# Cross-attention with layer norm on one core: another table of slots for weight sums, scalings, loads and output steps

## The chip, the cores and the metric

The kernel runs on one core of a Trainium2 chip. The metric is the device time of one execution in microseconds (us); the core's engines are TensorE (PE, with its weight loads PEld), VectorE (DVE), ScalarE (ACT), GpSimd (POOL) and SyncE (SP, which here only issues DMAs). All data are 32-bit floats, apart from a mask of bytes.

## The reference

Eight batches of 256 query rows (x, 1024 columns) attend to 256 context rows with 32 heads of 32 columns. Cut to what is computed:

```python
x = (hidden - mu) * rsqrt(var + 1e-5) * ln_gamma + ln_beta
Q = split_heads(x @ Wq.T)              # K = V = split_heads(ctx)
scores = einsum('bhsd,bhtd->bhst', Q, K) * 32 ** -0.5
probs = softmax(where(mask, scores, -inf))
attn = einsum('bhst,bhtd->bhsd', probs, V)
out = hidden + attn.reshape(B, S, 1024) @ Wout.T
```

## The kernel before, in words

**Slots.** The work of a batch is cut into eight groups of four heads (128 columns), so there are 64 groups, and the main loop has 64 slots n = 0 to 63. What slot n issues to PE, in this order: the scores of group n+1 (L596, 16 matmuls into four PSUM banks `sc`), output steps of place 0, the product of probabilities and values of group n-2 (L780, 64 matmuls), output steps of place 1, a piece of the query projection for a coming group (L455 for batches 0 to 2, L557 later), and output steps of place 2. Each engine takes its instructions in the order in which the program issues them; engines wait for each other by semaphores. From slot 1 on a slot takes PE 6.7 to 12 us. Slot 5 begins at 58.3 us of the span, slot 6 at 65.9, slot 7 at 73.4, slot 8 at 81.0, slot 9 at 90.0, slot 17 at 157.4, slot 23 at 213.1, slot 41 at 366.3.

**Softmax of a group** (`softmax_parts`, called in slot n for group n+1). For each of four heads j and two halves of the rows: DVE reads the scores from PSUM, adds the mask and takes the minimum (L636, the scores are negated), ACT takes the exponential and its sum (L640). Then, per head, `normalize(j)`: DVE takes the reciprocals of both sums (L650), and two instructions scale the halves of the tile `e` by them, 128x256 each (L656 on POOL or DVE, L654 on ACT). A pair (n, j) of the table `scaled` names the engine, A, V or P; pairs that the table does not list are POOL's. Then `blocks(j)`: DVE transposes the tile in blocks of 32 into `pT` (L662), and ACT copies a part (`aside`, L668). The order on DVE is exponentials of heads 0, 1, 2, `normalize(0)`, those of head 3, `normalize(1)`, `blocks(0)`, `normalize(2)`, `blocks(1)`, `normalize(3)`, `blocks(2)`; in groups below 8 `blocks(3)` comes in the next slot, behind the first two reads of scores. The scores of a group go into the four banks that the group before must have left, so scores n+1 wait until DVE has read scores n. Four DMAs on SP's queue then swap parts of `pT` among partitions.

**Weights.** After the first batch the query weights are multiplied by gamma, one of eight folds for each block of 128 outputs (L476, POOL; `foldat` has the slot of each). Query product 15, which slot 8 issues, needs fold 7 of slot 7. From batch 3 on the query projection, and the output projection of all batches, use seven products of half size in place of eight (a Strassen-Winograd scheme). For this the weights are summed: T1 = B12 - B11, T3 = B22 - B12, T2 = T3 + B11, T4 = B21 - T2, each in four chunks of 128x512, for the query weights by `sum_wq` (L506, table `wq`: slot, name, chunk, engine), for the output weights by `sum_wo` (L292, table `wo`: slot, name as a number, 3 for T1 to 6 for T4, chunk, engine). Sums and folds are issued at the end of a slot, behind the slot's softmax. T1, T3 and B11 of the query weights are stored to memory (`keeps`) and loaded into a ring again for each batch (`rings`).

**Layer norm.** x is loaded, DVE takes the statistics (L341, L344, L346), POOL the power -1/2 (L349), the row block is normalised by POOL or DVE (L367) or ACT (L362, with a shift from POOL, L359); `norm2` has the engines for batch 2's two row blocks. DVE transposes blocks (L426) and sixteen DMAs move them among partitions (`move_x`). The sums of x for the products are POOL's (L545).

**Output.** Steps of the output projection (L870, one chunk of one product, two matmuls of 128x512 in the profile) are spread over nine slots and three places by the tables `st0` (batch 0) and `stg` (batches 2 to 5); DVE adds results to the residual rows (L908, L912), POOL adds a product kept aside (L903), the rows go out by DMA.

**DMA queues.** `qp` names loads, moves and stores that POOL's queue issues instead of SP's: 1 at once, 2 at the end of the slot (`while at_end`). A key like `k%4` stands for all key loads of groups 24 to 55 with n % 8 = 4. `vearly` moves a value load into the slot before, at one of three places of SP's order.

All tables are one dictionary, PLAN, at the top of the file. The order was written out by this planner's table; nothing is decided while the kernel runs. The place of the sums and folds in the loop:

```python
        for o in FOLDS_AT.get(n, ()):
            fold(o, ENGINES[PLAN.get("folds", "PPPPPPPP")[o]])
        for one in sums[n]:
            one()
        while at_end:
            at_end.pop(0)()
```

Of the kernel before, what the change touches and what calls it, by code (L numbers as in the profile page):

```python
# [33 lines left out]


# [1 line left out]
PLAN = {'wq': [[9, 'T1', 0, 'P'], [14, 'T1', 1, 'V'], [15, 'T1', 3, 'P'], [14, 'T1', 2, 'P'], [16, 'T3', 2, 'V'],  # L37
# [13 lines left out]
 'folds': 'PPPPPPPP',  # L51
 'b2': {'loads': [0, 0],
        'stats': [2, 3],
        'norms': [2, 3],
        'trans': [4, 5],
        'moves': [5, 5, 5, 5, 5, 5, 6, 6, 6, 6, 6, 6, 7, 7, 7, 7]},
 'b3': {'loads': [-14, -11],
        'stats': [-10, -9],
        'norms': [-8, -7],
        'trans': [-7, -6],  # L60
        'moves': [-6, -6, -6, -6, -5, -5, -5, -5, -4, -4, -4, -4, -4, -4, -3, -3]},
 'norm2': 'PA',
 'norm3': 'AA',
 'SPLIT': 3,
 'rings': [[-3, -4], [0, 0], [2, 2]],
 'foldat': [-1, 0, 3, 3, 4, 5, 6, 7],
 'st0': [0, 0, 0, 0, 6, 2, 0, 0, 1, 0, 3, 2, 0, 2, 0, 0, 0, 2, 0, 2, 2, 0, 2, 0, 0, 4, 0],
 'stg': [0, 0, 0, 0, 5, 3, 0, 0, 4, 0, 0, 1, 0, 3, 0, 0, 0, 3, 0, 1, 4, 0, 0, 1, 0, 3, 0],
 'rel': {'loads': [-13, -12],
         'stats': [-11, -9],  # L70
         'norms': [-9, -8],
         'trans': [-8, -6],
         'moves': [-6, -6, -6, -6, -6, -6, -6, -5, -5, -5, -5, -4, -4, -4, -4, -4]},
 'woload': [[0, 0, 3], [3, 1, 1], [3, 0, -1], [0, 1, 1], [2, 0, 2], [2, 1, 2]],
 'n11': 'V',
 'p1late': [0, 3],
 'qp': {'out00': 2,
        'out01': 2,
        'out10': 2,
# [6 lines left out]
        'mv2_13': 2,  # L86
        'mv2_7': 2,
        'r1_01': 2,
        'mv15': 1,
        'x1None': 2,  # L90
        'mv3_2': 2,
        'k%4': 1,
        'v56': 2,
        'keptT31': 1},
 'vearly': {'30': 'z',
            '44': 'b',
            '54': 'a',
            '34': 'z',
            '56': 'a',
            '6': 'z',  # L100
            '10': 'b',
            '62': 'z',
            '12': 'z',
            '48': 'a',
            '2': 'z',
            '58': 'a',
            '26': 'b',
            '8': 'a',
            '28': 'z',
            '32': 'b',  # L110
            '52': 'z',
            '42': 'b',
            '38': 'z'},
 'rs': [0, 1, 1, 0],
 'rs0': [0, 0, 2, 3]}

# [15 lines left out]
P = 128  # L132
# [7 lines left out]
def xattn_kernel(  # L140
# [29 lines left out]
    xp = ctx.enter_context(tc.tile_pool(name="xp", bufs=2))  # L170
    rp = ctx.enter_context(tc.tile_pool(name="rp", bufs=PLAN.get('bufs',{}).get('rp',4)))
    lnp = ctx.enter_context(tc.tile_pool(name="lnp", bufs=2))
    kp = ctx.enter_context(tc.tile_pool(name="kp", bufs=2))
    vp = ctx.enter_context(tc.tile_pool(name="vp", bufs=PLAN.get('bufs',{}).get('vp',2)))
    atp = ctx.enter_context(tc.tile_pool(name="atp", bufs=3))
    ep = ctx.enter_context(tc.tile_pool(name="ep", bufs=PLAN.get('bufs',{}).get('ep',4)))
    ptp = ctx.enter_context(tc.tile_pool(name="ptp", bufs=PLAN.get('bufs',{}).get('ptp',3)))
    asp = ctx.enter_context(tc.tile_pool(name="asp", bufs=PLAN.get('bufs',{}).get('asp',3)))
    up = ctx.enter_context(tc.tile_pool(name="up", bufs=1))
# [23 lines left out]
    xs, ks, vs, rs = {}, {}, {}, {}  # L203
    QP = PLAN.get('qp', {})
    at_end = []
# [1173 lines left out]
```

## Time and profile before

| what | us |
|---|---|
| median of three runs | 575.13 |
| lowest and highest run | 574.39, 576.4 |
| the profiled execution, whole | 575.16 |
| its span, first to last instruction | 573.4 |

| engine | busy, share of the span |
|---|---|
| TensorE, matmuls | 99% |
| TensorE, weight loads | 69% |
| VectorE | 81% |
| ScalarE | 75% |
| GpSimd | 70% |

A line of the page or of the trace reads: line of the kernel, engine, operation, tile written <- tiles read, shapes, count, and then times. In a line of the timeline the first two numbers are the start and the length in us, and a bracket at the end has the idle time of the engine before it and what ended that. In a line of waits stand the waiting engine and line, what it waited for, the total in us, the number of waits and the longest. In a line of groups stand, behind the count, the busy time in us and the mean of one in ns. Where a line's instructions are asked for by source, three numbers are the shortest, the median and the longest in ns, with the first and the last start. In a line of stretches stand the limits, the length, and the busy time of PE, PEld, DVE, ACT and POOL (the counts beside PE, PEld, DVE, ACT, POOL in brackets), the granted clock of PE, the share of the DMA engines and GB/s. Matmuls overlap, and their ends are modelled, so a busy PE is not always a PE at its peak.

### The profile page before, as it was taken

To read this page: it belongs to the slowest core of one execution; us is meant where nothing else is said; L and a number is where in the kernel's file an instruction comes from. 1 tells how busy PE (TensorE), PEld (TensorE's weight loads), DVE (VectorE), ACT (ScalarE), POOL (GpSimd) and SP (SyncE) were. 2 spreads that over 40 slices of the span, in tenths; PEclk is the share of its full clock that TensorE was granted. 3 is DMA by queue.
4 is the path that set the end of the run, shared out by engine and by line. 5 is a ranking of instruction groups with operands and counts; after the bars stand their busy time and mean duration, and the time that the engine had idled before them with its cause. 6 is when DMAs were issued, how large, how long until landed. Compare 5 with 4: busy or idle time off the path is not lost.

```text
span 573.4 us, 19969 instructions
## 1 busy us (share of the span) xinstructions
PE 565.7 (99%) x7162; PEld 393.4 (69%) x7162; DVE 466.9 (81%) x1704; ACT 431.5 (75%) x1480; POOL 398.9 (70%) x653
## 2 busy tenths in 40 slices
PE   8999999999999999999999999999999999999997
PEld 7788875766667776677776677667766776755544
DVE  5998899888969889988888887888977787779823
ACT  3698978778779867888578877789767787869820
POOL 2678888888686994976668764696647576458780
PEclk9999999999999999999999999999999999999999
DMA  8767877656788677886788667967687666455741
GB/s 303 272 188 249 261 182 195 183 170 188 180 241 264 186 201 220 224 231 197 206 245 240 180 203 213 270 188 222 181 236 212 177 178 201 130 166 150 205 146 74
DMA packets 45283, 116.93 MB, mean 204 GB/s; under 512 B 9072, under 2 KB 9840, under 8 KB 45184
## 3 DMA queue, kind: packets, MB, share of 16 engines
q1 hardware_dynamic: 41312, 103.64, 63.2%
q0 software_dynamic: 3584, 12.00, 6.8%
q8 instruction: 57, 0.93, 0.7%
q14 instruction: 42, 0.34, 0.2%
q10 hardware_dynamic: 288, 0.01, 0.0%
HBM read 64.23 MB, written 11.53 MB: 132 GB/s over the span
## 4 chain that ended last, share of the span: by engine, by line
PE 63%; POOL 12%; DVE 10%; ACT 5%; issue 4%; DMA 3%; SPq 1%; DVEq 0%; POOLq 0%
PE po_S L870 13%; PE pq_A L557 12%; PE po_A L870 8%; PE sc L596 8%; POOL e L656 8%; PE pv L780 7%; PE pq_S L557 5%; PE pq L455 5%; DVE e L636 4%; ACT e L640 3%; DVE pT L662 3%; PE po_end L937 2%; DMA pT<-pT 2%; POOL wo L292 1%; DMA wq<-in_wq_dram 1%
## 5 line engine op out<-in xcount | busy, mean ns | idle before, releaser
L656 POOL TENSOR_SCALAR e<-e,rden 128x256 f32<-128x256 f32 x456 | 210.2, 476 | 129.7 <-DVE rden L650 123.1
L640 ACT ACTIVATE e<-e,mn 128x256 f32<-128x256 f32 x512 | 254.0, 501 | 43.5 <-DVE mn L636 43.4
L662 DVE STREAM_TRANSPOSE pT<-e 128x512 f32<-128x512 f32 x256 | 180.5, 707 | 56.4 <-POOL e L656 34.2
L636 DVE CUSTOM_DVE_ANT_0 e<-sc,mb 128x256 f32<-128x256 f32 x512 | 185.1, 415 | 16.5 <-PE sc L596 16.4
L668 ACT COPY pc<-pT 128x512 f32<-128x512 f32 x128 | 79.0, 617 | 57.5 <-DVE pT L662 37.4
L640 ACT ACTIVATION_READ_ACCUMULATOR e<-e,mn 128x1 f32 x512 | 97.8, 191 | 0.0
L455 PE MATMUL pq<-xnT,wq 128*128 128x256 f32 (+1 forms) x368 | 84.5, 383 | 0.8 <-POOL wq L476 0.8
L455 PEld LDWEIGHTS pq<-xnT,wq 128*128 128x128 f32 x368 | 68.6, 190 | 15.3 <-issue 4.1
L870 PE MATMUL po_S<-wo,at 128*128 128x512 f32 x152 | 73.8, 609 | 0.7 <-DVE r L912 0.7
L780 PE MATMUL pv<-pT,v 64*32 64x128 f32 x4096 | 74.2, 274 | 0.0
L596 PE MATMUL sc<-k,qa 32*128 32x256 f32 x1024 | 74.1, 401 | 0.1
L596 PEld LDWEIGHTS sc<-k,qa 32*128 32x128 f32 x1024 | 46.4, 184 | 39.2 <-issue 20.6
L780 PEld LDWEIGHTS pv<-pT,v 64*32 64x32 f32 x4096 | 57.0, 105 | 22.9 <-issue 13.8
L870 PE MATMUL po_A<-wo,at 128*128 128x512 f32 x128 | 58.2, 601 | 0.5 <-DVE qa L573 0.3
L870 PE MATMUL po_S<-wo,s 128*128 128x512 f32 x104 | 47.9, 597 | 0.0
L557 PEld LDWEIGHTS pq_A<-xnT,wq 128*128 128x128 f32 x352 | 40.7, 192 | 4.1 <-issue 3.2
L636 DVE DVE_READ_ACCUMULATOR2_ANT mn<- 128x1 f32 x512 | 42.2, 82 | 0.0
L870 PEld LDWEIGHTS po_S<-wo,at 128*128 128x128 f32 x152 | 26.0, 189 | 23.5 <-issue 22.2
L870 PEld LDWEIGHTS po_A<-wo,at 128*128 128x128 f32 x128 | 23.3, 190 | 27.4 <-issue 25.2
L557 PE MATMUL pq_A<-xnT,wq 128*128 128x128 f32 x352 | 41.5, 276 | 0.0
L650 DVE RECIPROCAL rden<-den 128x2 f32<-128x2 f32 x256 | 37.2, 145 | 3.0 <-ACT e L640 2.3
L793 ACT COPY at<-pv 128x128 f32<-128x128 f32 x128 | 26.1, 253 | 8.7 <-PE pv L780 8.7
(111 smaller groups left out, 654.8 us busy)
## 6 DMA issues: line engine op xcount, KB each, us to landing
pT<-pT SPq DMA_DIRECT2D x128, 128.0 KB, 3.1
pT<-pc SPq DMA_DIRECT2D x128, 128.0 KB, 3.8
v<-in_kv_dram SPq DMA_DIRECT2D x31, 512.0 KB, 5.2
ring<-kept_T SPq DMA_DIRECT2D x15, 512.0 KB, 5.7
k<-in_kv_dram SPq DMA_DIRECT2D x28, 256.0 KB, 4.0
r<-in_x_dram SPq DMA_DIRECT2D x27, 256.0 KB, 5.4
xnT<-xe SPq DMA_DIRECT2D x89, 64.0 KB, 2.9
x<-in_x_dram SPq DMA_DIRECT2D x11, 512.0 KB, 4.9
```

What stands on the lines that cost most here:

```text
L455: nc.tensor.matmul(pqs[n], wq[:, o, c, :], xnTs[b](c), start=(c == 0), stop=(c == NC - 1),)
L557: nc.tensor.matmul(pqs[b][:, o, :], w[:, c], x_[:, c], start=begins and o + c == 0, stop=c == NK - 1, skip_group_check=True,)
L596: nc.tensor.matmul(scs[n][j][:, s, :], qa[r, n % NQ, ts(s, P)], ks[n - n % 2][r, n % 2, :], start=True, stop=True,)
L636: nc.vector.tensor_tensor_reduce(out=e[:, s, :], in0=pss[j][:, s, :], in1=mbs[n // NQ], scale=1.0, scalar=NO_SCORE, op0=ALU.add, op1=ALU.m ...
L640: nc.scalar.activation(e[:, s, :], e[:, s, :], AF.Exp, bias=mn[:, s : s + 1], scale=-1.0, accum_out=den[:, s : s + 1],)
L650: nc.vector.reciprocal(rden, dens[j])
L656: engine.tensor_scalar(es[j][:, s, :], es[j][:, s, :], rden[:, s : s + 1], 1.0, ALU.mult, ALU.mult,)
L662: nc.vector.transpose(pT[:, :, :, j, :, :].rearrange("p a i s k -> p (a i) s k"), es[j].rearrange("p s (b t) -> p b s t", t=K),)
L668: nc.scalar.copy(pc[:, :, ts(j, 2)], pT[:, 1, :, ts(j, 2)])
L780: nc.tensor.matmul(pvs[n][r][j * HD : (j + 1) * HD], vs[n - n % 2][ts(r, 2 * K), n % 2, i, ts(j, HD)], pT[ts(r, 2 * K), :, i, j, :, :], st ...
L793: nc.scalar.copy(ats[b, k][:, c, :, ts(r, 2), :], pv.rearrange("p a s k -> p s a k"))
L870: nc.tensor.matmul(po, operand(b, name)[:, c], wo[:, which, c], start=begins and c == 0, stop=c == NK - 1, skip_group_check=not begins,)
```

## The change

Only PLAN changes. In the core of the diff, which leaves out value and row loads and the tables of `woload`:

```diff
- 'wq': [[9, 'T1', 0, 'P'], [14, 'T1', 1, 'V'], [15, 'T1', 3, 'P'], [14, 'T1', 2, 'P'], [16, 'T3', 2, 'V'],
-        [15, 'T3', 0, 'P'], [20, 'T2', 0, 'P'], [16, 'T3', 1, 'P'], [20, 'T2', 1, 'P'], [18, 'T3', 3, 'P'], ...
+ 'wq': [[9, 'T1', 0, 'V'], [15, 'T1', 3, 'V'], [14, 'T1', 2, 'P'], [16, 'T3', 2, 'V'], [15, 'T3', 0, 'V'],
+        [14, 'T1', 1, 'V'], [20, 'T2', 0, 'P'], [15, 'T3', 1, 'P'], [20, 'T2', 1, 'P'], [21, 'T4', 1, 'P'], ...
- 'wo': [[4, 5, 1, 'P'], [6, 4, 1, 'V'], [13, 3, 1, 'P'], [3, 5, 2, 'P'], [4, 5, 0, 'P'], [10, 6, 1, 'P'],
-        [5, 5, 3, 'P'], [11, 6, 2, 'P'], [8, 4, 2, 'P'], [14, 3, 3, 'P'], [10, 4, 3, 'V'], [12, 3, 2, 'P'],
-        [7, 4, 0, 'P'], [12, 6, 3, 'P'], [10, 6, 0, 'P'], [13, 3, 0, 'V']],
+ 'wo': [[4, 5, 1, 'P'], [6, 4, 1, 'V'], [11, 3, 1, 'P'], [4, 5, 0, 'P'], [3, 5, 2, 'P'], [10, 6, 1, 'P'],
+        [10, 4, 3, 'V'], [5, 5, 3, 'V'], [8, 4, 2, 'P'], [7, 4, 0, 'P'], [11, 6, 2, 'P'], [14, 3, 3, 'P'],
+        [12, 3, 2, 'P'], [10, 6, 0, 'P'], [13, 3, 0, 'P'], [11, 6, 3, 'P']],
- 'keeps': [[15, 'T1', 0], [16, 'T1', 1], [17, 'T3', 0], [19, 'T3', 1], [11, 'B11', 0], [13, 'B11', 1]],
- 'rings2': [0, 2],
+ 'keeps': [[16, 'T1', 0], [16, 'T1', 1], [18, 'T3', 0], [19, 'T3', 1], [11, 'B11', 0], [14, 'B11', 1]],
+ 'rings2': [1, 2],
- scaled: [40, 1, 'A'], [6, 0, 'A'], [18, 2, 'A'], [4, 2, 'A']
+ scaled: [15, 0, 'A'], [8, 2, 'A'], [4, 3, 'A'], [19, 2, 'A'], [12, 3, 'A'], [52, 0, 'A'], [11, 2, 'A'],
+         [29, 2, 'A'], [59, 3, 'A'],
+         [56, 0, 'V'], [37, 0, 'V'], [19, 0, 'V'], [25, 2, 'V'], [6, 1, 'V'], [37, 2, 'V']
- 'norm2': 'PA',
+ 'norm2': 'VA',
- 'foldat': [-1, 0, 3, 3, 4, 5, 6, 7],
- 'st0': [0, 0, 0, 0, 6, 2, 0, 0, 1, 0, 3, 2, 0, 2, 0, 0, 0, 2, 0, 2, 2, 0, 2, 0, 0, 4, 0],
- 'stg': [0, 0, 0, 0, 5, 3, 0, 0, 4, 0, 0, 1, 0, 3, 0, 0, 0, 3, 0, 1, 4, 0, 0, 1, 0, 3, 0],
+ 'foldat': [1, -1, 3, 4, 1, 5, 6, 7],
+ 'st0': [0, 0, 0, 0, 4, 4, 0, 0, 3, 0, 1, 1, 0, 3, 0, 0, 1, 0, 0, 3, 3, 0, 1, 0, 0, 4, 0],
+ 'stg': [0, 0, 0, 0, 7, 1, 0, 0, 4, 0, 0, 0, 0, 4, 0, 0, 0, 4, 0, 0, 4, 0, 0, 1, 0, 3, 0],
- 'p1late': [0, 3],
+ 'p1late': [3, 4, 5],
- qp: 'mv15': 1, 'v56': 2
+ qp: 'v56': 1, 'k%2': 2, 'keptT11': 1, 'mv2_6': 2, 'ring7_B111': 2, 'mv7_14': 1, 'mv7_11': 2, 'out1_10': 2
```

In words: three sums of weights net go from POOL to DVE (T1[0], T1[3] and T3[0] of the query weights; of the output weights T3[3] in slot 5 goes to DVE and T1[0] in slot 13 back to POOL), others change their slot; of the 256 pairs of scalings 39 are not POOL's, in place of 28, and six of those 39 are DVE's, each of two instructions; one row block's normalisation of batch 2 goes to DVE; three folds change their slot; output steps, stores of kept weights and ring loads move by a slot or so; ten DMAs more and three fewer are issued by POOL, among them the key loads of groups 26, 34, 42 and 50. Value loads come a slot earlier for more groups, the residual rows of the first batch come earlier, and single moves of x among partitions go to a neighbouring slot (one of batch 2 earlier and one later, one of each batch from 3 on later). No matmul is added or removed.

More of the change, by code (lines that the diff above doesn't have):

```diff
@@ L36 @@
 import math
-PLAN = {'wq': [[9, 'T1', 0, 'P'], [14, 'T1', 1, 'V'], [15, 'T1', 3, 'P'], [14, 'T1', 2, 'P'], [16, 'T3', 2, 'V'],
[2 rows of a table removed]
+PLAN = {'wq': [[9, 'T1', 0, 'V'], [15, 'T1', 3, 'V'], [14, 'T1', 2, 'P'], [16, 'T3', 2, 'V'], [15, 'T3', 0, 'V'],
[2 rows of a table added]
         [20, 'T2', 3, 'P']],
[10 rows of a table removed]
[11 rows of a table added]
  'folds': 'PPPPPPPP',
@@ L55 @@
         'trans': [4, 5],
-        'moves': [5, 5, 5, 5, 5, 5, 6, 6, 6, 6, 6, 6, 7, 7, 7, 7]},
+        'moves': [5, 5, 5, 5, 5, 6, 6, 6, 6, 6, 6, 6, 6, 7, 7, 7]},
  'b3': {'loads': [-14, -11],
@@ L60 @@
         'trans': [-7, -6],
-        'moves': [-6, -6, -6, -6, -5, -5, -5, -5, -4, -4, -4, -4, -4, -4, -3, -3]},
- 'norm2': 'PA',
+        'moves': [-6, -6, -6, -6, -5, -5, -5, -5, -4, -4, -4, -4, -4, -3, -3, -3]},
+ 'norm2': 'VA',
  'norm3': 'AA',
@@ L72 @@
          'trans': [-8, -6],
-         'moves': [-6, -6, -6, -6, -6, -6, -6, -5, -5, -5, -5, -4, -4, -4, -4, -4]},
- 'woload': [[0, 0, 3], [3, 1, 1], [3, 0, -1], [0, 1, 1], [2, 0, 2], [2, 1, 2]],
+         'moves': [-6, -6, -6, -6, -6, -6, -6, -5, -5, -5, -4, -4, -4, -4, -4, -4]},
+ 'woload': [[3, 1, 2], [3, 0, -1], [2, 0, 2], [2, 1, 1], [0, 0, 3], [0, 1, 2]],
  'n11': 'V',
- 'p1late': [0, 3],
+ 'p1late': [3, 4, 5],
  'qp': {'out00': 2,
@@ L88 @@
         'r1_01': 2,
-        'mv15': 1,
         'x1None': 2,
@@ L92 @@
         'k%4': 1,
-        'v56': 2,
-        'keptT31': 1},
+        'v56': 1,
+        'keptT31': 1,
+        'k%2': 2,
+        'keptT11': 1,
+        'mv2_6': 2,
+        'ring7_B111': 2,
+        'mv7_14': 1,
+        'mv7_11': 2,
+        'out1_10': 2},
  'vearly': {'30': 'z',
@@ L97 @@
             '54': 'a',
-            '34': 'z',
-            '56': 'a',
+            '34': 'b',
             '6': 'z',
@@ L102 @@
             '62': 'z',
-            '12': 'z',
-            '48': 'a',
+            '12': 'b',
             '2': 'z',
-            '58': 'a',
+            '58': 'z',
             '26': 'b',
-            '8': 'a',
             '28': 'z',
@@ L112 @@
             '42': 'b',
-            '38': 'z'},
+            '36': 'b',
+            '46': 'z',
+            '40': 'b',
+            '24': 'z',
+            '14': 'a',
+            '38': 'a',
+            '48': 'b',
+            '60': 'a',
+            '50': 'z',
+            '4': 'a'},
  'rs': [0, 1, 1, 0],
- 'rs0': [0, 0, 2, 3]}
+ 'rs0': [-1, -2, 1, 3]}
 from contextlib import ExitStack
```

15 rows, old and new, of the table PLAN are left out of this document.

## The prediction

> **What bounds the kernel now.** I read the head of the page, then the busy time of each engine in stretches of the span, then the list of what TensorE (PE) waited for.
>
> ```profile
> span 573.4 us, 19969 instructions
> PE 565.7 (99%) x7162; PEld 393.4 (69%) x7162; DVE 466.9 (81%) x1704; ACT 431.5 (75%) x1480; POOL 398.9 (70%) x653
> ```
> ```profile
> 50.80:99.50 48.70, 47.71 (x617) 35.23 (x616) 42.81 (x156) 40.82 (x140) 42.19 (x61) 1.00 0.75 210
> ```
> ```profile
> 230.30:366.30 136.00, 136.00 (x1845) 96.55 (x1844) 115.87 (x423) 107.13 (x369) 93.77 (x162) 1.00 0.78 220
> 366.30:537.70 171.40, 171.12 (x2299) 114.38 (x2298) 139.51 (x534) 136.69 (x478) 115.83 (x202) 1.00 0.67 187
> ```
> ```profile
> PE pq L455 <- POOL wq L476: 0.8, 1, 0.8
> PE po_S L870 <- DVE r L912: 0.7, 1, 0.7
> PE po_A L870 <- DVE qa L573: 0.3, 1, 0.3
> PE po_A L870 <- ACT qa L464: 0.2, 1, 0.2
> ```
>
> The columns of a stretch are its length, then the busy time of PE, its weight loads, VectorE (DVE), ScalarE (ACT) and GpSimd (POOL). PE is busy in 136.00 of 136.00 us in slots 25 to 40 and in all but 0.3 us of the next 171. Its clock is 1.00 in every stretch. The change adds and removes no matmul, so it can only give or take PE's waits. Inside the loop these are four, 2.0 us together, and they stand in slots 8, 9, 23 and 41; the rest of the list is of the head and the tail. A busy PE hides part of a wait (the ends of matmuls are modelled), so I followed the one that matters through slots 6 to 8:
>
> ```profile
> 73.41 1.15 PE L596 MATMUL sc<-k,qa 32*128 32x256 f32 x16
> 75.46 1.93 POOL L476 TENSOR_TENSOR wq<-wq,gs 128x1024 f32<-128x1024 f32 x1
> 75.56 2.37 DVE L292 TENSOR_TENSOR wo<-wo 128x512 f32<-128x512 f32 x1
> 77.86 0.41 DVE L636 CUSTOM_DVE_ANT_0 e<-sc,mb 128x256 f32<-128x256 f32 x1
> 80.95 1.59 PE L596 MATMUL sc<-k,qa 32*128 32x256 f32 x16
> 83.30 0.15 DVE L650 RECIPROCAL rden<-den 128x2 f32<-128x2 f32 x1
> 84.44 1.90 POOL L476 TENSOR_TENSOR wq<-wq,gs 128x1024 f32<-128x1024 f32 x1
> 86.39 3.72 PE L455 MATMUL pq<-xnT,wq 128*128 128x256 f32 x16 [0.80 <-POOL wq L476]
> ```
>
> The scores take 1.15 us in slot 7 and 1.59 us in slot 8: PE has to wait there, 0.44 us, for DVE to have read the banks of the softmax before. After that the query product waits for fold 7 on POOL: the eight matmuls ahead of it start at 83.60 and need 1.99 us at most, it starts at 86.39. Their own pace is 8 x 0.22 = 1.8 us (the sixteen after them take 3.72), so the hole is about 1.0. With slot 9's wait that is 1.4 + 0.2 us. The origin is one row higher: the sum of output weights in slot 6, on DVE, takes 2.37 us, because it was issued 0.10 us behind fold 6 on POOL, and ends 0.54 us after that (77.93 against 77.39). The whole softmax of slot 8 stands behind it on DVE, and fold 7 behind that softmax's scalings on POOL.
>
> **The change, part by part.** First the prices.
>
> ```profile
> 63.03 2.52 POOL L292 TENSOR_TENSOR wo<-wo 128x512 f32<-128x512 f32 x2
> ```
> ```profile
> L656 POOL TENSOR_SCALAR e<-e,rden 128x256 f32<-128x256 f32 x456 | 210.2, 476 | 129.7 <-DVE rden L650 123.1
> ```
> ```profile
> L292 DVE TENSOR_TENSOR wo<-wo x3: 1003/1344/2373, 75.6 to 134.1; 128x512 f32<-128x512 f32 x3
> ```
> ```profile
> L506 DVE TENSOR_TENSOR wq<-wq x4: 651/679/680, 161.4 to 215.5; 128x512 f32<-128x512 f32 x4
> L506 DVE TENSOR_TENSOR ring<-wq x1: 1751/1751/1751, 143.2 to 143.2; 128x512 f32<-128x512 f32 x1
> ```
> ```profile
> L654 ACT ACTIVATE e<-e,rden 128x256 f32<-128x256 f32 x56 | 25.1, 499 | 2.3 <-DVE rden L650 2.2
> L367 POOL TENSOR_SCALAR x<-x,mv,rstd 128x1024 f32<-128x1024 f32 x1 | 3.8, 3779 | 0.1
> L367 DVE TENSOR_SCALAR x<-x,mv,rstd 128x1024 f32<-128x1024 f32 x4 | 3.2, 795 | 0.0
> L215 POOL DMA_DIRECT2D k<-in_kv_dram x4 | 2.4, 604 | 0.0
> ```
>
> *POOL's account.* Eleven pairs of scalings leave it (28 pairs elsewhere before, 39 after): 22 x 0.476 = 10.5 us. Three weight sums net go to DVE: 3 x 2.52 / 2 = 3.8. One row of layer norm goes: 3.8. Ten more DMA issues come (four key loads, three moves, one store of weights, one ring load, one output row) and three go (move 15): 7 x 0.6 = 4.2. Net -13.9 us, on an engine that idles 129.7 us before its scalings, 123.1 of them waiting for DVE's reciprocals. So POOL's relief is no time by itself; it counts only where DVE waits for POOL.
>
> *DVE's account.* It gets six pairs of scalings, three sums and one norm. A DVE scaling of 128x256 is not in the trace: the norm of 128x1024, the same operation, takes 0.795, so one lies between 0.2 (a quarter) and 0.8; I take 0.3, near the quarter, since the fixed part is small. Six pairs are 3.6 us, the norm 0.8, the sums 0.65 to 2.4 each. DVE is the next busiest engine, and where slots are short it has no room: 42.81 of 48.70 us.
>
> *Slots 1 to 4.* Folds 0 and 4 now stand together in slot 1 (2 x 1.9 us, where POOL idles before its next scaling) and the norm of slot 2 runs on DVE: about 0.6 + 0.8 us later on DVE. I cost it at nothing, because in slot 4 the second reciprocal waits for ACT, which has a norm of its own there; if that cover went, 1.4 us would arrive at slot 8. Slot 3 loses a fold, which starts POOL's scalings there 1.9 us sooner, behind the same wait for ACT.
>
> *Slots 5 to 8.* These decide.
>
> ```profile
> 68.52 1.90 POOL L476 TENSOR_TENSOR wq<-wq,gs 128x1024 f32<-128x1024 f32 x1
> ```
> ```profile
> 64.33 0.17 DVE L650 RECIPROCAL rden<-den 128x2 f32<-128x2 f32 x1
> ```
> ```profile
> 66.11 0.71 DVE L662 STREAM_TRANSPOSE pT<-e 128x512 f32<-128x512 f32 x1 [0.48 <-ACT e L654]
> 68.25 0.71 DVE L662 STREAM_TRANSPOSE pT<-e 128x512 f32<-128x512 f32 x1 [0.73 <-ACT e L654]
> 68.89 0.39 DVE L636 CUSTOM_DVE_ANT_0 e<-sc,mb 128x256 f32<-128x256 f32 x1
> 71.94 0.42 DVE L636 CUSTOM_DVE_ANT_0 e<-sc,mb 128x256 f32<-128x256 f32 x1
> ```
>
> Behind the reciprocal at 64.33 DVE now does the scaling pair (6,1): 2 x 0.3 us, and some 0.4 in front of it, since POOL is at two sums until 63.03 + 2.52 = 65.55 (or, relieved before, a little less): +1.0, between 0.4 (two of 0.2, no wait) and 2.0 (two of 0.8 and the wait). The pair (6,0) leaves ACT for POOL, so the wait of 0.48 goes: -0.5. The one of 0.73 stays, since (6,2) is still ACT's. At 68.89, ahead of the next softmax, now stands the sum T3[3] (POOL's before), beside fold 5, which starts at 68.52: it costs 0.65 if it comes ahead of the fold and 2.4 behind it; I take the mean of the three such sums on DVE, 1.6, since the two requests fall within a few tenths. Together +2.1 us for every exponential of softmax 7, between 0.5 and 3.9. Scores 8 (73.41) need the last of them read, which is at 72.36 today: 1.05 us of slack, so PE waits 1.05 in slot 7. In slot 8 there is no slack, PE already waits, and the other 1.05 arrives there. Softmax 8 moves along, because POOL's scalings of softmax 7 wait for reciprocals, not for the sum that POOL lost. The new pair (8,2) on ACT does not bring fold 7 forward: POOL's last scaling before it waits for the reciprocal at 83.30, and 83.37 + 2 x 0.476 = 84.3 against 84.44. **Slots 5 to 8: +2.1.**
>
> The Trainium skill, SBUF — State Buffer, section "Who interferes with whom", says that a GpSimd instruction and a VectorE one with two SBUF inputs hold a shared pair of ports exclusively: whichever is issued first keeps it to its end, and the other stands still. The trace agrees with 77.93 against 77.39. By that rule, T3[3] behind fold 5 would cost 1.9 + 0.5 = 2.4 us instead of 1.6, and the time would be 578.0.
>
> *Slots 9 to 17.*
>
> ```profile
> 156.35 0.42 DVE L636 CUSTOM_DVE_ANT_0 e<-sc,mb 128x256 f32<-128x256 f32 x1
> ```
> ```profile
> 157.44 0.93 PE L596 MATMUL sc<-k,qa 32*128 32x256 f32 x12
> ```
>
> T1[0] goes to DVE in slot 9, T1[0] of the output weights back to POOL in slot 13 (1.00 us), and T1[3] and T3[0] to DVE at the end of slot 15, with T3[1] on POOL beside them. Softmax 17 is behind these; its last read ends at 156.77, 0.67 before PE wants the bank. Two sums are 1.3 to 3.5 us, less the 1.0 given back in slot 13: 0.3 to 2.5 against 0.67 of slack, so nothing to 1.8 us. The four uncontended sums are the nearest rows (0.68), which leaves next to nothing; with T3[1] beside them I put **+0.3**. In slot 17 POOL loses a sum ahead of its scalings; DVE waits there, PE does not.
>
> *Slot 41.*
>
> ```profile
> 357.78 0.71 DVE L662 STREAM_TRANSPOSE pT<-e 128x512 f32<-128x512 f32 x1 [1.06 <-ACT e L654]
> ```
>
> ACT has pairs (40,1) and (40,2) behind its exponentials, and DVE waits 1.06 us for the first. It goes back to POOL, which is idle there; the wait of 0.3 us for L573 in slot 41, later on the same chain, goes: **-0.3**. Slot 23's wait (0.7, L912 behind three sums in slot 22, which stay) remains.
>
> *The rest.* Between the rows of scores below lies the shortest kind of slot; a chain row gives the matmuls of the output projection.
>
> ```profile
> 248.94 1.08 PE sc L596 x16
> ```
> ```profile
> 255.73 1.08 PE sc L596 x16
> ```
> ```profile
> 526.60 3.63 PE po_A L870 x8
> ```
>
> Output steps moved within a batch leave PE's sum as it is. The shortest slot, 6.8 us, loses one step (two matmuls of 0.45) and falls to 5.9, while DVE needs 115.87 / 16 = 7.2 on average, of 136 / 16 = 8.5 given. That backlog of 1.3 us is made up in the slots that grow; without this cover it would cost up to 0.9 us a batch. The four key loads are issued on POOL's queue at the end of a slot, behind its scalings, and are used more than a slot later, so the later landing is hidden, and SP's queue is shorter by what POOL's took; value and row loads come earlier. The five further pairs on ACT (net) and the five on DVE in slots 18 to 55 meet DVE's spare 1.3 us a slot. Nothing.
>
> **The sum.** +2.1 + 0.3 - 0.3 = +2.1 us. The profiled execution took 575.16 (its span and 1.8 us around it), the median of the three runs is 575.13, so they can be taken for one another: **577.2**. The bounds: 0.5 + 0 - 0.3 = +0.2 and 3.9 + 1.8 - 0 = +5.7.
>
> **The rivals.** *DVE gets ahead (faster).* One mechanism, in slot 6: the sum there was issued 0.10 us behind fold 6. If the change lets DVE issue first, 2.37 becomes about 0.65, softmax 8 comes 1.7 us earlier, and the waits of slots 8 and 9 go. With slot 41 that is -1.4 - 0.2 - 0.3 = -1.9: **573.2**. For it: the margin is a tenth of a microsecond, and POOL has 13.9 us less to do. Against: the sum follows a transpose that follows POOL's third scaling and a mask bias, and the fold follows the fourth scaling, so the order is built in.
>
> *Everything is hidden.* The new DVE work falls into waits for POOL and ACT that it shortens as it fills them, T3[3] comes ahead of fold 5, and slot 7's slack takes the rest: the lower bound, +0.2, **575.4**. For it: DVE idles 5.9 of 48.7 us in that stretch. Against: those waits are mostly behind, not ahead of, the place where the work lands. The Trainium skill, Perfetto Trace Analysis, section "Optimizing Scalar/DVE Operations", says that moving operations between GpSimd and VectorE may not help since they share a read port; no gain either, and 0.48 and 1.06 us of this trace's waits are of another kind, ACT's.
>
> *Both collisions.* T3[3] behind fold 5 and slot 15's pair beside T3[1]: +0.8 and +1.5 on top of the forecast: **579.5**.
>
> **How the numbers follow.** Forecast (576 to 578.6) 0.38, ahead 0.28, hidden 0.22, both collisions 0.12. A difference below 0.3%, 1.7 us, is about what a measurement of this kernel can't tell from no change, so the limits are 573.4 and 576.9. Of the forecast's 0.38 I put 0.08 below 576.9. Faster 0.28; same 0.22 + 0.08 = 0.30; slower 0.30 + 0.12 = 0.42. The forecast's own range is 576 to 578.6. The range for 8 in 10 goes from 572.6, into the faster case, to 579.4; it leaves out the upper bound of +5.7.
>
> **What would show it.** In the profile after, the DVE sum of output weights in slot 5 stands behind fold 5 and takes over 1.3 us, scores 8 and 9 take longer than 1.15 us, and PE still waits for fold 7. If the sum in slot 6 takes under 1 us, the first rival is right. If slot 17's scores wait, the third. A PE wait after 230 us, where there is none, would make the step on output steps and key loads wrong.

## The result, and the profile after

The changed kernel takes 577.8 us (median of six runs, 576.98 to 579.22), the kernel before 574.92 in six runs beside it: ratio 1.0048, 95% interval 1.0031 to 1.0065. The prediction was 577.2, slower. Time and sign hold; what follows shows that most of the terms that they were made of do not. The profiled execution took 577.87, its span is 576.1 (before: 575.16 and 573.4).

The list of what PE waited for in the changed kernel, without the waits of the head (waiting engine and line; what released it; total us, times, longest). Line numbers are 13 higher than before.

```profile
PE po_A L883 <- DVE qa L586: 0.9, 1, 0.9
PE pq_A L570 <- ACT xnT L580: 0.7, 1, 0.7
PE pv L793 <- ACT pc L681: 0.6, 1, 0.6
PE po_A L883 <- ACT qa L477: 0.5, 1, 0.5
PE pq L468 <- POOL wq L489: 0.4, 1, 0.4
PE po_A L883 <- ACT p L891: 0.4, 1, 0.4
...
PE pv L793 <- issue: 0.3, 1, 0.3
```

Two of before's four waits are gone from it: the residual rows of slot 23 (L912 before) and slot 41's L573 (L586 now, which stands in the list for slot 25). Fold 7 (now L489) is still waited for, half as long. Five entries are new; the two largest, L586 in slot 25 and L580 in slot 37, stand where PE never waited. The stretches, cut at the same slots as before, show where PE idles (length; PE, PEld, DVE, ACT, POOL; clock; DMA share; GB/s):

```profile
50.85:100.35 49.50, 47.68 (x617) 35.06 (x617) 44.26 (x161) 41.60 (x142) 38.70 (x57) 1.00 0.83 231
231.05:369.17 138.12, 136.48 (x1841) 97.02 (x1841) 119.04 (x432) 107.76 (x371) 92.35 (x159) 1.00 0.76 214
369.17:540.39 171.22, 171.17 (x2295) 114.61 (x2295) 139.67 (x534) 137.67 (x480) 113.81 (x197) 1.00 0.68 191
```

The clock is 1.00 throughout. PE is idle 1.6 us in slots 25 to 40, where before it was idle for 0.00, and the stretch is 2.1 us longer.

To place each loss, I take a slot's length, from its first scores to those of the next slot, and subtract PE's own time for the same matmuls, read from slots without a wait (slot 7 before: 80.95 - 73.41 = 7.54 us). This is good to some 0.02 us a slot, and output steps that only move drop out of it. Each column is one profiled execution; the right one is the last experiment.

| slots | before, us lost | after | last version |
|---|---|---|---|
| 5 and 6 | 0.0 | 1.3 | 0.0 |
| 7 and 8 | 1.5 | 0.7 | 0.1 |
| 9 and 10 | 0.3 | 0.8 | 0.3 |
| 17 | 0.2 | 0.8 | 0.2 |
| 19, 21, 23 | 1.2 | 0.3 | 0.3 |
| 25 and 26 | 0.0 | 1.1 | 0.0 |
| 37 and 39 | 0.1 | 1.1 | 0.1 |
| 41 | 0.3 | 0.0 | 0.0 |
| 55 | 0.1 | 0.3 | 0.1 |
| 2 to 61 together | 3.6 | 6.2 | 0.9 |

The last row holds the other slots too, each of them at about -0.01. Its 2.6 us are the difference of the spans (2.7).

**Slots 5 to 8 in the trace.** VectorE in the changed kernel (start, length, idle time before in brackets):

```profile
64.35 0.17 DVE L663 RECIPROCAL rden<-den 128x2 f32<-128x2 f32 x1
64.55 0.84 DVE L669 TENSOR_SCALAR e<-e,rden 128x256 f32<-128x256 f32 x2
...
68.16 0.71 DVE L675 STREAM_TRANSPOSE pT<-e 128x512 f32<-128x512 f32 x1 [0.32 <-ACT e L667]
68.79 0.65 DVE L305 TENSOR_TENSOR wo<-wo 128x512 f32<-128x512 f32 x1
69.36 0.41 DVE L649 CUSTOM_DVE_ANT_0 e<-sc,mb 128x256 f32<-128x256 f32 x1
```

And GpSimd's two folds of slots 5 and 6:

```profile
68.83 2.37 POOL L489 TENSOR_TENSOR wq<-wq,gs 128x1024 f32<-128x1024 f32 x1
...
75.95 1.93 POOL L489 TENSOR_TENSOR wq<-wq,gs 128x1024 f32<-128x1024 f32 x1
```

T3[3] (68.79) was issued 0.04 us ahead of fold 5 (68.83), so it took 0.65, and the fold 2.37 in place of 1.90: the side that comes second is held up. The scaling pair costs 0.84, and the two waits for ACT shrink together by 0.89 (0.48 and 0.73 before, the second 0.32 now). Softmax 7 starts at 69.36 against 68.89: 0.47 late, not 2.1. In slot 6 nothing changed: the sum there is still 0.10 behind its fold, and that 0.5 us is how late fold 7 arrives (84.94 against 84.44; PE goes on at 86.89 against 86.39):

```profile
76.05 2.37 DVE L305 TENSOR_TENSOR wo<-wo 128x512 f32<-128x512 f32 x1
```
```profile
84.94 1.90 POOL L489 TENSOR_TENSOR wq<-wq,gs 128x1024 f32<-128x1024 f32 x1
```

Slot 8 itself loses less than before, because PE comes to it 1.3 us later: it had waited in slot 5, for probabilities that the DMAs were still swapping among partitions. The list puts part of that wait down to ACT's copy, but the two swaps issued from 50.80 on land 8.9 and 9.3 us after their issue, the second at 60.7, and PE goes on at 60.78:

```profile
60.78 1.13 PE L793 MATMUL pv<-pT,v 64*32 64x128 f32 x62 [0.61 <-ACT pc L681]
```

### The profile page after: what moved, and what is told of

The parts are those of the page before. It is cut to its first block, busy times and chain, and to the rows that moved or that the text cites. A ratio compares the mean times of both kernels' runs of the same rounds, so it can differ in the third digit from the quotient of the medians.

```text
span 576.1 us, 19962 instructions
## 1 busy us (share of the span) xinstructions
PE 567.2 (98%) x7162; PEld 394.7 (69%) x7162; DVE 474.2 (82%) x1720; ACT 435.2 (76%) x1490; POOL 386.1 (67%) x634
## 4 chain that ended last, share of the span: by engine, by line
PE 64%; DVE 14%; ACT 8%; POOL 6%; issue 4%; DMA 3%; SPq 0%; DVEq 0%; POOLq 0%; ACTq 0%
PE po_S L883 14%; PE pq_A L570 12%; PE po_A L883 9%; PE sc L609 8%; PE pv L793 7%; PE pq_S L570 6%; DVE e L649 5%; POOL e L669 5%; ACT e L653 4%; DVE pT L675 4%; PE pq L468 3%; PE po_end L950 2%; DMA pT<-pT 2%; ACT e L667 2%; PE busy L213 1%
## 5 line engine op out<-in xcount | busy, mean ns | idle before, releaser
L669 POOL TENSOR_SCALAR e<-e,rden 128x256 f32<-128x256 f32 x434 | 200.2, 476 | 145.5 <-DVE rden L663 139.7
L883 PE MATMUL po_S<-wo,at 128*128 128x512 f32 x152 | 72.1, 606 | 0.2
```

Of the source, the lines that this page charges most:

```text
L669: engine.tensor_scalar(es[j][:, s, :], es[j][:, s, :], rden[:, s : s + 1], 1.0, ALU.mult, ALU.mult,)
L883: nc.tensor.matmul(po, operand(b, name)[:, c], wo[:, which, c], start=begins and c == 0, stop=c == NK - 1, skip_group_check=not begins,)
```

## The experiments

The theory after the two traces: the loss comes from VectorE's new scalings, which stand still when GpSimd has a sum of two tiles in hand; the wait in slot 5 comes from the loads, and a chain on VectorE and GpSimd up to fold 7 absorbs it. The rivals are in the expectations. Each run's median stands with its ratio to runs of the kernel before on the same chip.

**1. Loads back.** After, with

```diff
- 'woload': [[3, 1, 2], [3, 0, -1], [2, 0, 2], [2, 1, 1], [0, 0, 3], [0, 1, 2]],
+ 'woload': [[0, 0, 3], [3, 1, 1], [3, 0, -1], [0, 1, 1], [2, 0, 2], [2, 1, 2]],
- vearly: '4': 'a'
```

> The changed kernel (577.8) with the loads of output weights back in their slots of before (two each in slots 1 and 2 in place of one and three) and the value load of group 4 no longer a slot early. All agree that TensorE's 0.9 us of waits in slot 5 come from the swaps of pT landing late among these loads, so slot 5's loss of 1.28 us goes. Theory 'one chain': VectorE and POOL did not wait for TensorE in slots 5 to 8, so fold 7 ends when it ended, and the wait moves to slot 8: slot 8's loss grows from 0.69 to about 1.9, slots 5 to 10 together stay at 2.8 +- 0.3, time 577.7. Rival 'losses add up': slots 5 to 10 lose 1.5, time 576.5. Second rival, the swaps are late for another reason: slot 5 keeps 1.2 or more, time 577.8.

Measured: 578.3 us, ratio 1.005 (1.0033 to 1.0067). Slot 5 loses nothing, so the second rival falls. But slot 6 loses 2.0 where nobody expected a loss, and there PE waits for the value load that is late again:

```profile
PE pv L792 <- DMA v<-in_kv_dram: 1.8, 1, 1.8
```

Slot 8 then loses 0.4. The 1.3 us taken out of slot 5 gave no time back, but because of the new wait this run doesn't show what the chain alone would have taken.

**2. Only the value load back.** After, with

```diff
- vearly: '4': 'a'
```

> The changed kernel with only the value load of group 4 back in its slot of before (slot 4, not 3). If the three loads of output weights in slot 2 are what delays the swaps of pT, slot 5 still loses 0.8 to 1.3 us. If the early value load is, slot 5 loses nothing. In both cases the chain theory gives 577.7, the theory that losses add up 577.7 and 576.5.

Measured: 577.8 us, ratio 1.0045 (1.003 to 1.0061). Slot 5 loses 2.9 and slot 6 0.8, slots 7 to 10 nothing. This run differs from run 1 by `woload` alone, so the three loads in slot 2 cause slot 5's wait; and the early value load was what kept slot 6 whole. The swaps of `pT` that slot 5 needs, issued from 46 to 53 us, show the delay, first in run 1, then in this run (KB each, median us from issue to landing):

```profile
pT<-pc SPq DMA_DIRECT2D x2, 128.0 KB, 6.0
```
```profile
pT<-pc SPq DMA_DIRECT2D x2, 128.0 KB, 10.3
```

In the fourteen profiled executions of this case, all five with three loads in slot 2 and the value load early lose 1.2 to 4.7 us in slot 5, and none of the eight with two loads there waits for a swap in it; three of the five with the late value load lose 0.8 to 2.5 in slot 6, and none of the nine with the early one.

**3. No scalings on VectorE.** After, with

```diff
- scaled: [56, 0, 'V'], [37, 0, 'V'], [19, 0, 'V'], [25, 2, 'V'], [6, 1, 'V'], [37, 2, 'V']
```

> The changed kernel with the six pairs of scalings of VectorE back on POOL. Theory 'VectorE's scaling is held by a POOL instruction with two tiles read': the 1.95 us scaling in slot 25 and the 1.35 us one in slot 37 go, and with them the losses of slot 25 (1.0 us) and slot 37 (0.76 us); slots 5 to 10 change by less than 0.4; time 576.1. Rival 'output steps moved': slots 25 and 37 lose the same as now, because slots 27 and 35 have become short (5.93 us), time 577.8. Rival from the prediction: VectorE's spare time hides the pairs, so that their removal brings nothing, 577.8.

Measured: 574.77 us, ratio 0.9998 (0.9982 to 1.0013): 3.0 us below the changed kernel, all of its loss. Slots 25, 37 and 39 lose nothing, slot 55 0.07. The profiled execution, 576.67, is one of the slowest of the ten; it lost 1.6 us in slots 40 and 42 waiting for DMAs, which the median, 1.9 us shorter, probably did not. The six pairs are worth more than the 1.7 expected, and the rival that blames the moved output steps falls, since they are all still here.

**4. Slot 16's sum.** After, with

```diff
- wq: [16, 'T3', 2, 'V']
+ wq: [16, 'T3', 2, 'P']
```

> The changed kernel with the sum T3[2] of slot 16 on POOL in place of VectorE. In the changed kernel it took 1.77 us, behind a sum of x that POOL had begun 0.07 us before; in the kernel before it took 0.65. Theory 'slot 17 lost by this collision': slot 17's loss falls from 0.81 to 0.2 or less, time 577.2. Rival, the prediction's step (the pair T1[3], T3[0] on VectorE at the end of slot 15): slot 17 still loses 0.6 or more, time 577.7.

Measured: 577.21 us, ratio 1.0036 (1.0024 to 1.0048); slot 17 loses 0.18. The collision is the cause, the pair in slot 15 is not. In the changed kernel, DVE and then POOL at the end of slot 16, and DVE's same sum before:

```profile
162.56 1.77 DVE L519 TENSOR_TENSOR wq<-wq 128x512 f32<-128x512 f32 x1
```
```profile
162.49 1.29 POOL L558 TENSOR_TENSOR sx<-xnT 128x512 f32<-128x512 f32 x1
```
```profile
161.40 0.65 DVE L506 TENSOR_TENSOR wq<-wq 128x512 f32<-128x512 f32 x1
```

Before, POOL's sum of x waited for a move and came 2 us behind DVE; in the changed kernel SP issues the last of these moves some 3.6 us earlier (156.97 against 160.56), and the sum comes 0.07 us ahead.

**5. Two of the six pairs to POOL.** After, with

```diff
- scaled: [25, 2, 'V'], [37, 2, 'V']
```

> The changed kernel with two of VectorE's six pairs of scalings, (25,2) and (37,2), back on POOL; (6,1), (19,0), (37,0) and (56,0) stay. Theory 'held by a POOL sum': only these two pairs met a sum of POOL with two tiles read, so slots 25, 37 and 39 lose nothing more (-1.0, -0.8, -0.3): 575.7. Rival 'VectorE's work itself': four of six pairs are still there, so about two thirds of what all six cost (3.0 us by the run without them) stay: 576.8.

Measured: 576.17 us, ratio 1.0024 (1.0013 to 1.0035), between the two. By slots the theory is right: 25, 37 and 39 lose nothing. The four remaining pairs still cost 1.4 against run 3; the profiles place 0.2 of it in slot 55 and 0.6 in slots 5 to 10, and leave 0.6 unplaced (this profiled execution, 577.74, lost 1.4 in slots 40 and 42, as run 3's did).

**6. The six pairs alone.** Before, with

```diff
+ scaled: [56, 0, 'V'], [37, 0, 'V'], [19, 0, 'V'], [25, 2, 'V'], [6, 1, 'V'], [37, 2, 'V']
```

> The kernel before with nothing but the six pairs of scalings added on VectorE. Theory 'the six pairs are the loss': slot 25 loses 1.0 and slot 37 about 0.8 us where before lost nothing, and the pair (6,1) makes slots 8 and 9 lose 0.4 to 0.9 more: 577.2 to 578.0. Rival 'the pairs hurt only beside the other edits' (POOL's emptier queue, the shorter slots 27 and 35): 575.1 to 575.6.

Measured: 578.28 us, ratio 1.005 (1.0033 to 1.0067): 3.3 us, more than the whole change, from twelve instructions. Slots 25 and 26 lose 1.1, slot 37 0.75, slot 55 0.2 more, slots 7 and 8 lose 2.8 against 1.5: the pair (6,1), without the relief from ACT and with its first scaling held to 1.15 us behind a sum on GpSimd, costs 1.3. The pairs need no other edit to hurt.

**7. Slot 6's sum on POOL.** Before, with

```diff
- wo: [6, 4, 1, 'V']
+ wo: [6, 4, 1, 'P']
```

> The kernel before with the sum T2[1] of output weights of slot 6 on POOL in place of VectorE, where it took 2.37 us behind fold 6. It prices the prediction's first rival (VectorE not held in slot 6). If the waits of slots 8 and 9 come from that sum, they shrink from 1.8 to 0.4 us or less, since POOL's sum ends before it scales again: 573.7. If fold 7 is late for another reason (POOL's own work, which grows by 1.3 us), slots 8 and 9 still lose 1.2 or more: 574.6 to 575.2.

Measured: 574.68 us, ratio 0.9995 (0.9981 to 1.0009), inconclusive. Slots 7 to 10 lose nothing, as expected, but this execution lost 2.5 us in slot 6 to the value load, and so it doesn't show whether the sum or the late PE emptied them:

```profile
PE pv L780 <- DMA v<-in_kv_dram: 2.3, 1, 2.3
```

**8. A first combination.** After, with the edits of runs 3 and 4, run 1's `woload`, and

```diff
- wo: [6, 4, 1, 'V']
+ wo: [6, 4, 1, 'P']
```

> The changed kernel with the six pairs of scalings on POOL, the sums T2[1] of slot 6 and T3[2] of slot 16 on POOL, and the loads of output weights in their slots of before (the value load of group 4 stays a slot early). If the losses found so far are separate and complete, slots 5 to 10 lose 0.8 or less, slot 17 0.2, slot 23 0.4, slots 25, 37, 39 and 55 nothing: 572.3. If the chain of slots 5 to 8 has another link that comes last, slots 5 to 10 lose 1.5 to 2.5: 573.5.

Measured: 575.01 us, ratio 0.9998 (0.9989 to 1.0008), a miss of 2.7 (and 1.5 above the second branch's 573.5). Slots 5 and 6 lose nothing, but 7 and 8 lose 2.1, as in the second branch. The pair (6,0), back from ACT on POOL, stands behind two sums there, VectorE waits 0.85 us for it, and does T3[3] after that. 1.0 us more went in slots 40 and 42 of the profiled execution.

**9. Slot 6's sum with the value load early.** Before, with

```diff
- wo: [6, 4, 1, 'V']
+ wo: [6, 4, 1, 'P']
+ vearly: '4': 'a'
```

> The kernel before with T2[1] of slot 6 on POOL and the value load of group 4 in slot 3. In the run with the sum alone TensorE lost 2.5 us in slot 6 to that value load, which hid what the sum is worth. If the two are the first links of slots 5 to 9, slots 5 to 10 lose 0.3 or less in place of 1.8 and nothing else changes: 573.5. If the value load only moves the delay to the swaps of pT ahead of it, slot 5 loses 1 us or more and the time is 574.5 to 575.

Measured: 573.34 us, ratio 0.9979 (0.9968 to 0.999), as expected and faster than both kernels. Slots 5 to 10 lose 1.3 in the profiled execution (574.18, above the median) against 1.8 before, more than the 0.3 expected: the chain is shorter, not gone. That profile is 1.0 us shorter than before's; 0.5 of it lies in these slots, and 0.5 ahead of slot 5, which the edit doesn't explain.

**10. A second combination.** Run 8, with

```diff
+ scaled: [6, 0, 'A']
- wo: [5, 5, 3, 'V']
+ wo: [5, 5, 3, 'P']
```

> The changed kernel with the six pairs of scalings off VectorE, T3[2] of slot 16, T2[1] of slot 6 and T3[3] of slot 5 on POOL, the pair (6,0) on ACT as before, and the loads of output weights as before with the value load of group 4 in slot 3. The run without the last two lost 1.1 and 1.0 us in slots 7 and 8, where VectorE waited 0.85 us for the pair (6,0) on POOL and then did T3[3]. If these two links are the rest, slots 5 to 10 lose 0.5 or less, slots 17 and 23 0.5 together: 572.8. If POOL with both sums is the next link, slots 7 and 8 still lose 1 us or more: 574.

Measured: 574.2 us, ratio 0.9988 (0.9979 to 0.9997): the second branch. Slots 7 and 8 lose 1.4, half of it waiting for fold 7 on POOL. Slot 5 loses 0.65 waiting for a fold of slot 4; POOL came to it late, since it had waited 3.3 us for a load of output weights before the sum ahead of it.

**11. The same six pairs, two of them one head earlier.** After, with

```diff
- scaled: [25, 2, 'V'], [37, 2, 'V']
+ scaled: [25, 1, 'V'], [37, 1, 'V']
```

> The changed kernel with VectorE scaling heads 1 of groups 25 and 37 in place of heads 2; the number of VectorE's pairs stays six. Theory 'held by a POOL sum': at that place POOL has no sum waiting, the four instructions take 0.35 to 0.5 us each, slots 25, 37 and 39 lose nothing: 575.9 to 576.3, as in the run with the two pairs on POOL. Rival 'VectorE's work itself': the same work, the same loss, 577.8.

Measured: 575.66 us, ratio 1.0017 (1.0005 to 1.0029), 2.1 below the changed kernel, with the same number of instructions on every engine. Slots 25, 37 and 39 lose nothing. The twelve scalings on VectorE (shortest, median, longest ns), in the changed kernel and here:

```profile
L669 DVE TENSOR_SCALAR e<-e,rden x12: 347/354/1952, 64.6 to 493.5; 128x256 f32<-128x256 f32 x12
```
```profile
L669 DVE TENSOR_SCALAR e<-e,rden x12: 333/350/501, 64.9 to 493.4; 128x256 f32<-128x256 f32 x12
```

The medians are equal, the longest falls from 1952 to 501 ns. For these two pairs this rules out VectorE's amount of work. (The profiled execution, 577.8, lost 4.7 us in slot 5 to the swaps.)

**12. What the runs point to.** Run 10, with the early slots put back as they were before:

```diff
- wq: [9, 'T1', 0, 'V']
+ wq: [9, 'T1', 0, 'P']
- scaled: [8, 2, 'A'], [4, 3, 'A']
+ scaled: [4, 2, 'A']
- 'foldat': [1, -1, 3, 4, 1, 5, 6, 7], 'norm2': 'VA'
+ 'foldat': [-1, 0, 3, 3, 4, 5, 6, 7], 'norm2': 'PA'
- b2 moves: [5, 5, 5, 5, 5, 6, 6, 6, 6, 6, 6, 6, 6, 7, 7, 7], qp: 'mv2_6': 2
+ b2 moves: [5, 5, 5, 5, 5, 5, 6, 6, 6, 6, 6, 6, 7, 7, 7, 7]
```

> Slots 0 to 9 as in the kernel before with T2[1] on POOL and the value load of group 4 early (the run that took 573.34); from slot 10 on the changed kernel without its scalings on VectorE and with T3[2] of slot 16 on POOL. If the gains of the two halves add up, slots 5 to 10 lose 1.3, slots 17 and 23 0.5, slots 19, 21 and 41 nothing (0.7 less than before): 572.4. If the later slots only pay back what the first half saved, 573.3 or more.

Measured: 572.64 us, ratio 0.9964 (0.9951 to 0.9978), 2.5 us below the kernel before and 5.2 below the changed one, near the 572.4 of two gains that add up. Slots 5 to 10 lose 0.4, not the 1.3 that run 9's profile had with nearly the same early slots (the first batch's residual rows come early here too); whether those rows or the execution makes the difference is not shown. In the whole loop one wait is left on the list, beside the first and the last, which stand in the head and the tail:

```profile
PE busy L212 <- POOL ring masks.py:199: 1.4, 1, 1.4
PE po_end L949 <- ACT at L805: 0.3, 1, 0.3
PE po_A L882 <- ACT qa L476: 0.2, 1, 0.2
```

## Why the prediction was right, step by step

The time was right to 0.6 us by luck, because wrong terms nearly cancelled. By the table, slots 5 to 8 were put 1.6 too high (+0.5, not +2.1). Slots 9 to 17 were put 0.8 too low (+1.1, not +0.3), and the rest, put at nothing, 1.4 too low: the pairs in slots 25, 37, 39 and 55 cost 2.3, and slots 19 to 23 gave 0.9 back.

- **"Slots 5 to 8: +2.1."** The trace gives +0.5 (2.0 lost against 1.5). The parts: (6,1) was put at +1.0, with +0.84 in the trace (0.35 for a scaling alone, near the 0.3 that was taken) and 1.3 more lost in run 6; the waits for ACT fell by 0.9, not 0.5, because VectorE came later to the second one too; T3[3] was put at 1.6, the mean of three sums, and took its lower bound of 0.65, since it got ahead of fold 5 by 0.04 us. The mean was neither of the two outcomes that the prediction itself had named. The order was no coin toss either: in runs 1, 2, 4 and 5 the sum is ahead by 0.03 to 0.04 us again and takes 0.65; in run 11, where PE waits 4.7 us in slot 5, it comes while the fold is still running and takes 1.02. The tests named for this step say the same: the sum stands ahead of the fold, scores 8 and 9 take 1.15; only the wait for fold 7 is there.
- **"I cost it at nothing" (slots 1 to 4).** True of folds and norm as far as the trace shows: the reciprocal behind which (6,1) stands starts at 64.35, before at 64.33. The loads of output weights in these slots were not priced, and they delay the swaps that PE waits for in slot 5 (runs 1 and 2). It cost little: in after and runs 4 and 5, whose slots 5 to 8 are alike, those slots lose 2.0 together each time, whether slot 5 takes 1.2, 1.3 or 1.5 of it. The end of fold 7 sets the sum; a wait of PE ahead of it takes the place of the wait for it, as long as it is the shorter one. Run 11 has the same slots, and there the swaps cost slot 5 4.7 us and slots 6 to 8 nothing.
- **The pair (8,2) on ACT, put at no gain.** In the changed kernel VectorE waits 0.99 us for it at 84.94, and slot 9 loses 0.3 more. But in run 3 the same wait goes with 0.1 more, and in runs 8 and 10, which keep the pair on ACT, VectorE doesn't wait for it and slot 9 loses what it lost before. What the pair costs is not shown; no run tried it alone.
- **Slots 9 to 17, +0.3.** Slot 17 lost 0.6 more and slots 9 and 10 0.5 (slot 10's 0.25 has no cause on record), so the term was mis-sized, and slot 17 for another reason: the two sums in slot 15 ran in 0.68 and 0.69 us, and run 4 shows that T3[2] of slot 16 was the price.
- **Slot 41, -0.3.** Right: 0.34 to nothing.
- **Slot 23's wait, which "remains".** It fell from 1.0 to 0.4. In slot 22 VectorE has the mask bias, an instruction that reads one tile, beside a sum on GpSimd. Before, VectorE and GpSimd:

```profile
213.25 1.10 DVE L586 TENSOR_SCALAR mb<-mk 128x256 f32<-128x256 uint8 x1
```
```profile
212.91 1.28 POOL L846 TENSOR_TENSOR at<-at 128x512 f32<-128x512 f32 x1
```

After:

```profile
214.62 0.51 DVE L599 TENSOR_SCALAR mb<-mk 128x256 f32<-128x256 uint8 x1
```
```profile
213.71 1.27 POOL L859 TENSOR_TENSOR at<-at 128x512 f32<-128x512 f32 x1
```

Both end 0.15 us behind the sum, but before it was issued 0.94 us ahead of the sum's end and after 0.36. The 0.59 between the two lengths are as much as slot 23 gained. This is read from the two traces; no run tried it alone.

- **The five pairs on DVE in slots 18 to 55 "meet DVE's spare 1.3 us a slot": nothing.** This step failed. Spare time is an average; the pairs (25,2) and (37,2) stand where POOL begins a sum. In the changed kernel, VectorE and then GpSimd in slot 24:

```profile
229.96 2.36 DVE L669 TENSOR_SCALAR e<-e,rden 128x256 f32<-128x256 f32 x2
232.24 0.70 DVE L675 STREAM_TRANSPOSE pT<-e 128x512 f32<-128x512 f32 x1
```
```profile
230.24 0.62 POOL L228 DMA_DIRECT2D k<-in_kv_dram  x1
230.88 1.27 POOL L558 TENSOR_TENSOR sx<-xnT 128x512 f32<-128x512 f32 x1
```

Two scalings that take 0.62 in run 11 take 2.36 and end 0.16 us behind POOL's sum (232.31 against 232.15). Run 1 gave the counter-example by chance: there the sum waited for a move, VectorE was through before it began, and slot 25 lost nothing.

```profile
230.24 0.74 DVE L668 TENSOR_SCALAR e<-e,rden 128x256 f32<-128x256 f32 x2
```
```profile
231.48 1.27 POOL L557 TENSOR_TENSOR sx<-xnT 128x512 f32<-128x512 f32 x1 [0.33 <-DMA xnT<-xe]
```

- **Output steps and key loads, nothing.** Right for slots 25 and 37, though the test that was named would have it wrong: PE does wait after 230 us. Runs 3, 5 and 11 keep every moved step and key load and have no loss in slots 25 and 37. The test was badly chosen, since the pairs on VectorE could raise the same sign. Whether the moved loads are free in every execution stays open: of the ten profiles that start from the changed kernel, runs 3, 4, 5 and 8 lose 0.6 to 1.6 us in slots 28, 40 or 42, with a late ring load on the list of run 4 and a late swap on that of run 8, and none of the four that start from the kernel before loses anything there.
- **The rivals.** "DVE gets ahead" happened, but in slot 5, not in slot 6. Run 9, which takes slot 6's sum off VectorE and loads the value early, gains 1.5 us in its median, near the 1.6 that this rival gave that sum, but its profile places only 0.5 in slots 5 to 10. "Everything is hidden" named the right cause for slots 5 to 8 (T3[3] ahead of fold 5).

The Trainium skill, SBUF — State Buffer, section "Who interferes with whom", counts `tensor_scalar` among the operations that can take the pair shared with GpSimd. The prediction used this page for sums of two tiles only; the runs agree with the wider reading, with 0.35 us alone and 1.95 held. The Trainium skill, Perfetto Trace Analysis, section "Optimizing Scalar/DVE Operations", cited in the prediction as a reason for no gain, says that such a move may not help; run 6 gives the number here: six pairs moved from GpSimd to VectorE cost 3.3 us.

## What to carry to other kernels

When work moves from GpSimd to VectorE, look at what GpSimd has in hand at that very moment, not at VectorE's spare time: the same instruction took 0.35 or 1.95 us, and one head earlier it was free. Price an order that a tenth of a microsecond decides as two cases, never as their mean. And before a wait is called worth its length, look for the chain behind it: slot 5 lost 1.2, 1.3 or 1.5 us, and the slots up to fold 7 lost 2.0 each time; only a wait longer than the chain's own, 4.7 us in run 11, came through whole.

## What the runs showed of the hardware

- A scaling of one 128x256 tile on VectorE, with a single tile read from SBUF, takes 0.35 us alone, 0.48 to 0.57 beside scalings on GpSimd in the changed kernel, and 1.35 and 1.95 when a sum of GpSimd comes first. In slot 24 it stood from the end of the first scaling (229.96 + 0.48 = 230.44), 0.44 us before the sum's own start at 230.88, while GpSimd was issuing a DMA; in run 1, beside the same issue but with a sum that had to wait, it was not held. In runs 2, 4 and 6 the same scaling was held again, to 1.95, 1.95 and 1.96 us, each time from 0.43 to 0.45 us before the sum's start. The hold seems to begin when the sum is next in line; that is argued from these five executions, not tried.
- Landing times vary from one execution to the next: with the same order of loads in slots 2 to 4 and the value load late, slot 6 lost nothing before and in run 6, and 2.0 and 2.5 us in runs 1 and 7.
